# Decoder layer on one core: gather order, expert output buffers and the arithmetic of the last norms

## The chip, the cores and the metric

The kernel runs on one core of a Trainium2 chip. The metric is the time of one execution on the device in microseconds (us); lower is better. A core has five engines that run side by side and wait for each other through semaphores: TensorE (PE in the profile, its weight loads PEld), VectorE (DVE), ScalarE (ACT), GpSimd (POOL) and SyncE (SP), which here only starts transfers. Each engine works through its own queue in order: an instruction that waits holds all that are queued behind it.

## The reference, cut to what matters

One decoder layer on x of 16 x 100 tokens with 512 features: causal self-attention and a layer norm, cross-attention over 16 x 361 context tokens and a layer norm, then a mixture of experts and two norms. The change touches only that last stage:

```python
# x: layer norm of the cross-attention's residual, 1600 tokens x 512
logits = x @ router_w + router_b                  # 8 experts
topk_vals, topk_idx = top_k(logits, 2)
g = softmax(topk_vals)                            # two weights a token
c = sum_j g[j] * silu(x @ expert_w[e_j] + expert_b[e_j])
y = x + c @ proj_w + proj_b
y = norm_w * y / sqrt(mean(y * y) + 1e-6)         # RMS norm
x = x + y
out = (x - mean(x)) / sqrt(var(x) + 1e-5)         # layer norm
```

## The kernel before

Work goes by tiles of 128 tokens (`TT`, 13 tiles, the last of 64). Matrix products are done on pairs: a float32 operand is split into a high part h (a cast on ACT) and a low part l (the difference, on DVE or POOL), and `mm3` issues three matmuls (L145 to L147). `split` is where a pair is made (L137 the cast, L140 the difference).

The experts do not see every token. The gate finds each token's two experts, and each of the 3200 token-expert pairs is given a row in one of 32 slots (`NSL`) of 128 rows, each slot of one expert. The first 11 slots (`EARLY`) are settled before the gate has seen the last tiles; the indices of the others (`idx`, L1247) come later. For slot i:

- `e_gather` (L1261): an indirect DMA, issued by POOL, gathers 128 rows of x (`x2d` in memory) into a buffer of the pool `k_x`.
- `e_turn` (L1270): four PE transposes (tile pte), and the split into the pair xsT (two buffers).
- `e_product` (L1278): 12 matmuls into ph (two PSUM banks), with the expert's weights addressed by a register.
- `e_bias` (L1290): SP loads the expert's bias, broadcast over the partitions (three buffers).
- `e_out` (L1295): DVE adds the bias (L1298), ACT takes Silu (L1299), SP stores the rows to `ysd` in memory (L1300). The result h is written over the gathered rows, so that buffer is free only once the store has landed.

The final stage works on token tile t:

- `f_gather` (L1432): two indirect DMAs fetch the token's two expert rows from `ysd`. They need all slots before `upto(t)` stored: 19 slots for t up to 5, then two more with each tile.
- `f_load` (L1456): z (x plus the projection's bias) and x2.
- `f_sum` (L1475): the weighted sum, on ACT and DVE. `f_turn`, `f_split`: transposes ptc and the pair cp. `f_product`: 12 matmuls into pp.
- `f_square` (L1507): y = pp + z on DVE; ACT squares it and accumulates the sum (L1512); POOL multiplies y by norm_w in place (L1513), which has to come after the square has read y.
- `f_mean` (L1516), and then `f_norm` (L1608): for each step of the list `steps`, one vector of values `V2` goes through a root, `newton` for steps of the first six tiles (`REST`) and `roots` (Sqrt on ACT, a correction on DVE) for later ones. A step holds the RMS value of its own tile and the variance of the tile before. `f_first` adds x2 and takes mean and variance with bn_stats and bn_aggr; `f_second` applies the layer norm and stores.

Before the loop come `e_turn` and `e_product` of slots 0 to 2. The loop over i from 0 to 32 then issues, in program order, `e_gather(i + 4)`, `e_turn(i + 1)`, `e_product(i)`, `e_out(i)`, and what is due: the table `TURN` says in which iteration a final tile's `f_fetch` comes, and `f_prepare`, `f_project` and `f_norm` follow one iteration later each. Tiles from `LATE` on are gathered after the loop, into memory that the experts' weights leave.

The program order isn't the final order. A planner orders each engine's queue by planned times, within the dependencies. `in_turn` adds an order between two instructions of one engine without a semaphore, and `keep_in_program_order` keeps an instruction's place; the gathers have neither. `f_open`, at i = 12, loads and splits proj_w through the three buffers of the pool `stage`, which x2 and other loads use too.

Of the kernel before, what the change touches and what calls it, by code (L numbers as in the profile page):

```python
# [9 lines left out]
FP = mybir.dt.float32  # L10
FR = mybir.dt.float32r
AF = mybir.ActivationFunctionType
# [50 lines left out]
def tile_decoder_layer(  # L63
# [32 lines left out]
    def pool(stack, name, bufs=1, **k):  # L96
        return stack.enter_context(
            tc.tile_pool(name=name, bufs=bufs, reuse_waits="tile", **k)
        )
# [99 lines left out]
    def split_rows(dst, src, name, high=None, low=None):  # L199

        for k in range(KC):
            f = stage.tile([128, D], FP, name=f"f_{name}_{k}", tag="f")
            tc.keep_in_program_order(nc.sync.dma_start(f, src[:, k]))
            split(dst[:, k], f, high, low or nc.gpsimd)
# [7 lines left out]
    def kp(w):  # L212
        return w.rearrange("(k p) n -> p k n", p=128)
# [690 lines left out]
    fin = ExitStack()  # L904
    ctx.enter_context(fin)
    k1 = pool(fin, "k_1", 1, side="right")
    xsp = pool(fin, "k_x", 5, side="right")
    gs = ExitStack()
    gw = pool(gs, "gate", side="right")
    d_l = ExitStack()  # L910
# [347 lines left out]
    ew = Pair(WH, WL).rearrange("p e k n -> p (e k n)")  # L1258
    SLOT, XG, XS, PH = {}, {}, {}, {}

    def e_gather(i):  # L1261
        XG[i] = xsp.tile([128, D], FP, name=f"xs_{i}", tag="xs")
        nc.gpsimd.indirect_dma_start(
            out=XG[i][:],
            out_offset=None,
            in_=x2d[: CUT * 128] if i < EARLY else x2d[:],
            in_offset=bass.IndirectOffsetOnAxis(ap=SLOT[i][0], axis=0),
        )

    def e_turn(i):  # L1270
        xs = XG[i]
        pt = bank("t", [128, KC, 128], f"pte_{i}")
        for k in range(KC):
            nc.tensor.transpose(pt[:, k, :], xs[:, k * 128 : (k + 1) * 128], ident)
        XS[i] = pair(xsp, [128, KC, 128], f"xsT_{i}", tag="xsT", bufs=2)
        split(XS[i], pt)
# [9 lines left out]
        PH[i] = ph  # L1286

    EB = {}

    def e_bias(i):  # L1290
        rv = nc.sync.value_load(SLOT[i][2], min_val=0, max_val=(NE - 1) * D)
# [2 lines left out]

    def e_out(i):  # L1295
        ph = PH.pop(i)
        h = XG.pop(i)
        nc.vector.tensor_tensor(h, ph, EB.pop(i), ALU.add)  # L1298
        nc.scalar.activation(h, h, AF.Silu)  # L1299
        nc.sync.dma_start(ysd[i * 128 : (i + 1) * 128, :], h)  # L1300

    early = [1, 2, 4, 5]
# [107 lines left out]
    def f_open():  # L1410
        gs.close()
        inp["f1"] = pool(f_l, "f_1", 1, side="right")
        inp["f2"] = pool(f_l, "f_2", 3, side="right")
        inp["pw"] = pair(inp["f1"], [128, KC, D], "pw")
        split_rows(inp["pw"], kp(proj_w), "pw")
        inp["nw"] = inp["f1"].tile([128, D], FP, name="nw")
        nc.scalar.dma_start(inp["nw"], norm_w.partition_broadcast(128))

    F, L = {}, {}


    REST, LATE = 6, 8

    TURN = (19, 20, 21, 22, 24, 26, 28, 30)
    BEHIND = 2

    def upto(t):


        return min(NSL, max(EARLY + NE, 2 * (t + 1) + NE - 1))  # L1430

    def f_gather(t):  # L1432
        t0, n = TT[t]
        tail = t >= LATE
        if t == LATE:
            e_l.close()
            w_l.close()
            inp["f3"] = pool(f_l, "f_3", NT - t + 1)
        ys = []
        for j in range(2):  # L1440
            if tail:
                y = inp["f3"].tile([128, D], FP, name=f"y{j}_{t}", tag=f"y{j}")
            else:
                y = inp["f2"].tile([128, D], FP, name=f"y{j}_{t}", tag="y", bufs=6)
            nc.gpsimd.indirect_dma_start(
                out=y[:n],
                out_offset=None,
                in_=ysd[: upto(t) * 128],
                in_offset=bass.IndirectOffsetOnAxis(ap=slot[:n, j, t : t + 1], axis=0),
            )  # L1450
            ys.append(y)
        p = inp["f3" if tail else "f1"]
        cp = pair(p, [128, KC, 128], f"cp_{t}", tag="cp")
        F[t] = ys, cp

    def f_load(t):  # L1456
# [15 lines left out]
    def tiny(n, name, tag, dt=FP):  # L1472
        return inp.get("f3", small).tile([128, n], dt, name=name, tag=tag)

    def f_sum(t):  # L1475
        n = TT[t][1]
        c, y1 = F[t][0]
        tc.keep_in_program_order(
            nc.scalar.activation(c[:n], c[:n], AF.Copy, scale=g1[:n, t : t + 1])
        )  # L1480
        nc.vector.scalar_tensor_tensor(
            c[:n], y1[:n], g2[:n, t : t + 1], c[:n], ALU.mult, ALU.add
        )

    def f_turn(t):
        n = TT[t][1]
        (c, _), cp = F[t]
        pt = bank("s", [128, KC, 128], f"ptc_{t}")
        for k in range(KC):
            nc.tensor.transpose(  # L1490
                pt[:, k, :n], c[:n, k * 128 : (k + 1) * 128], ident[:n, :n]
            )
        F[t] = cp, pt

    def f_split(t):
        n = TT[t][1]
# [9 lines left out]

    def f_square(t):  # L1507
        n = TT[t][1]
        pp, (_, y) = F[t], L[t]
        nc.vector.tensor_tensor(y[:n], pp[:n], y[:n], ALU.add)  # L1510
        ss = tiny(1, f"yss_{t}", "yss")
        nc.scalar.activation(pp[:n], y[:n], AF.Square, accum_out=ss[:n])  # L1512
        nc.gpsimd.tensor_tensor(y[:n], y[:n], inp["nw"][:n], ALU.mult)  # L1513
        F[t] = ss

    def f_mean(t):  # L1516
        n = TT[t][1]
        k = 1.0 if t < REST else 0.25
        nc.vector.tensor_scalar(
            root(0, t)[:n], F[t][:n], k / D, k * EPS_RMS, ALU.mult, ALU.add  # L1520
        )


    steps = [([t], [t - 1] if t else []) for t in range(REST)]
    steps += [
        ([6], [5]),
        ([7, 8], [6]),
        ([9, 10], [7, 8]),
        ([11], [9, 10]),
# [10 lines left out]
    def root(j, t, of=V2):  # L1540

        i, k = where[j, t]
        if i not in V2:
            w = sum(map(len, steps[i]))
            V2[i] = tiny(w, f"sq_{i}", f"sq_{w}")
            if NT - 1 in steps[i][0] + steps[i][1]:
                nc.vector.memset(V2[i], 1.0)
        return of[i][:, k : k + 1]

    def f_first(t):  # L1550

        n = TT[t][1]
        v, r = root(0, t), root(0, t, R2)
        x2, y = L[t]


        if t < REST:
            s = tiny(1, f"s_{t}", "f_s")
            nc.vector.tensor_tensor(s, v, r, ALU.mult)
        else:  # L1560
            s = r
        nc.vector.scalar_tensor_tensor(y[:n], x2[:n], s[:n], y[:n], ALU.mult, ALU.add)  # L1562
        st = tiny(nc.vector.BN_STATS_DIM, f"st3_{t}", "ln_st")
        nc.vector.bn_stats(st[:n], y[:n])  # L1564
        mv = tiny(nc.vector.BN_AGGR_DIM, f"mv3_{t}", "ln_mv")
        nc.vector.bn_aggr(mv[:n], st[:n])
        nc.vector.scalar_tensor_tensor(
            root(1, t)[:n],
            v[:n],
            EPS_LN if t < REST else 4 * EPS_LN,  # L1570
            mv[:n, 1:2],
            ALU.mult,
            ALU.add,
        )
        F[t] = mv

    def f_second(t):
        t0, n = TT[t]
        r = root(1, t, R2)[:n]
        mv, (_, y) = F[t], L[t]  # L1580
        if t == NT - 1:
            nc.vector.tensor_scalar(  # L1582
                y[:n], y[:n], mv[:n, 0:1], r, ALU.subtract, ALU.mult
            )
        else:
            m = tiny(1, f"m3_{t}", "ln_m")
            nc.vector.scalar_tensor_tensor(  # L1587
                m[:n], mv[:n, 0:1], -1.0, r, ALU.mult, ALU.mult
            )
            nc.scalar.activation(y[:n], y[:n], AF.Identity, bias=m[:n], scale=r)  # L1590
        nc.sync.dma_start(out[t0 : t0 + n, :], y[:n])

    def f_fetch(t):
# [13 lines left out]

    def f_norm(i):  # L1608
        v = V2[i]
        if i < REST:  # L1610
            R2[i] = newton(v, f"f_{i}")
        else:
            R2[i] = roots(v, len(steps[i][0]), f"f_{i}")
        for t in steps[i][0]:
            f_first(t)
        for t in steps[i][1]:
            f_second(t)
# [43 lines left out]
    due = {}  # L1661
    for t in range(LATE):
        assert TURN[t] >= upto(t)
        for lag, f in enumerate((f_fetch, f_prepare, f_project, f_norm)):
            if t < REST or lag < 2:
                due.setdefault(min(TURN[t] + lag, NSL), []).append((lag, f, t))
    e_bias(TAIL)
    for i in range(NSL + 1):
        if i + 4 < NSL:
            e_gather(i + 4)  # L1670
        if TAIL < i + 1 < NSL:
            e_turn(i + 1)
            e_bias(i + 1)
        if TAIL <= i < NSL:
            e_product(i)
            e_out(i)
        if i == EARLY + 1:
            f_open()
        for _, f, t in sorted(due.get(i, []), key=lambda d: d[0]):
            f(t)  # L1680
    for t in range(LATE, NT):
        f_gather(t)
    done = REST
    for t in range(REST + 1, LATE):
        f_load(t)
    for k in range(REST, NT + 3):
# [88 lines left out]
```

## Time and profile before

| what | value |
|---|---|
| three runs, median (lowest to highest) | 1432.21 us (1428.25 to 1441.84) |
| the profiled execution, its own time | 1437.28 us |
| its span, first to last instruction | 1435.6 us |
| busy share of the span: PE, PEld | 93%, 77% |
| busy share of the span: DVE, ACT, POOL | 66%, 52%, 51% |
| mean granted TensorE clock | 0.973 |
| the gathers of x (L1263), first to last issue | 1218.8 to 1371.8 us |
| the gathers of expert rows (L1445) | 1322.1 to 1400.1 us |
| last PE matmul starts | 1419.3 us |

Busy shares are averages over all stages. The stages that the change doesn't touch (self-attention, cross-attention, gate) fill the first 1220 us. The change is to be judged in the last 220, stage by stage.

### The profile page before, as it was taken

What the parts mean: (1) busy time and instruction counts of PE and PEld (TensorE: products, weight loads), DVE (VectorE), ACT (ScalarE), POOL (GpSimd) and SP (SyncE); (2) the same over time, 40 slices, a digit from 0 to 9 for tenths busy, and PEclk for the clock granted to TensorE, in tenths of its full rate; (3) what the DMA queues carried; (4) which work ended last, traced back from release to release, by engine and by line L of the source; (5) the groups of instructions that cost most, each with busy time, mean ns of one, the idle gap of its engine ahead of it and who ended that gap; (6) DMA issues with size and microseconds to landing.
All of it is one profiled execution on the core that took longest, in us unless ns stands there. A gap on an engine that the chain in (4) does not pass through costs nothing. (4 is left out here: it accounts for less than half of the span.)

```text
span 1435.6 us, 25188 instructions
## 1 busy us (share of the span) xinstructions
PE 1342.1 (93%) x7952; PEld 1107.7 (77%) x7952; DVE 954.1 (66%) x2978; ACT 746.8 (52%) x1872; POOL 731.1 (51%) x854
## 2 busy tenths in 40 slices
PE   8999989999999999999999999999999897988884
PEld 6888878888778888888888888878887674666663
DVE  5766667775567777777777667767555559653698
ACT  4666643444436666566666566656553232332353
POOL 6877653443335555555555455545444445343542
PEclk9999999999999999999999999999999998899898
DMA  5221254555442232323233222223536554666674
GB/s 157 71 92 53 70 161 111 135 92 110 98 103 62 62 74 51 74 63 75 69 75 70 74 68 69 50 65 76 131 81 200 179 165 129 210 227 214 209 239 139
DMA packets 197873, 159.79 MB, mean 111 GB/s; under 512 B 133322, under 2 KB 152878, under 8 KB 197742
## 3 DMA queue, kind: packets, MB, share of 16 engines
q1 hardware_dynamic: 187904, 137.83, 36.2%
q0 software_dynamic: 4576, 14.95, 3.4%
q10 hardware_dynamic: 5262, 5.41, 1.3%
q8 instruction: 65, 1.06, 0.3%
q14 instruction: 66, 0.54, 0.1%
HBM read 107.16 MB, written 50.99 MB: 110 GB/s over the span
## 5 line engine op out<-in xcount | busy, mean ns | idle before, releaser
L759 POOL TENSOR_SCALAR p<-p,sums 100x361 f32<-100x361 f32 x256 | 146.4, 576 | 100.3 <-DVE sums L758 89.3
L746 DVE CUSTOM_DVE_ANT_0 p<-s,nmask 100x361 f32<-100x361 f32 x256 | 132.9, 527 | 64.7 <-PE s L147 56.2
L757 ACT ACTIVATE p<-p,nm 100x361 f32<-100x361 f32 x256 | 153.2, 602 | 39.8 <-DVE nm L746 36.5
L140 DVE TENSOR_TENSOR pT_l<-ptp,pT_h 128x400 fp32r<-128x400 f32 (+1 forms) x192 | 107.4, 567 | 59.3 <-ACT pT_h L137 58.8
L145 PE MATMUL pq<-WH 128*128 128x512 f32 (+2 forms) x272 | 106.5, 392 | 6.2 <-DVE WH L139 5.8
L767 PE MATMUL ptp<-ident,p 100*128 100x100 f32 (+1 forms) x768 | 107.6, 252 | 0.0
L140 POOL TENSOR_TENSOR cT_l<-cf,cT_h 128x512 fp32r<-128x512 f32 (+1 forms) x48 | 54.4, 1134 | 104.2 <-ACT cT_h L137 102.3
L137 ACT CAST pT_h<-ptp 128x400 fp32r<-128x400 f32 (+1 forms) x192 | 91.3, 487 | 30.2 <-PE ptp L767 29.7
L767 PEld LDWEIGHTS ptp<-ident,p 100*128 100x128 f32 (+1 forms) x768 | 95.6, 152 | 13.5 <-POOL p L759 2.3
L146 PE MATMUL pq<-WL,WH 128*128 128x512 f32 (+2 forms) x272 | 104.1, 383 | 0.0
L147 PE MATMUL pq<-WH,WL 128*128 128x512 f32 (+2 forms) x272 | 103.8, 382 | 0.0
L147 PE MATMUL acc<-WH,ot_l 128*128 128x512 f32 (+1 forms) x208 | 87.3, 421 | 8.7 <-DVE ot_l L140 6.9
L145 PE MATMUL acc<-WH,ot_h 128*128 128x512 f32 (+1 forms) x208 | 87.2, 419 | 5.5 <-ACT ot_h L137 5.5
L145 PE MATMUL s<-kT_h,WH 128*100 128x362 f32 x256 | 88.5, 356 | 2.4 <-ACT kT_h L137 2.4
L145 PE MATMUL av<-pT_h,WH 128*128 128x400 f32 (+1 forms) x192 | 77.1, 401 | 11.6 <-ACT pT_h L137 11.1
L146 PE MATMUL acc<-WL,ot_h 128*128 128x512 f32 (+1 forms) x208 | 85.1, 409 | 0.0
L147 PE MATMUL s<-kT_h,WL 128*100 128x362 f32 x256 | 84.5, 330 | 0.0
L146 PE MATMUL s<-kT_l,WH 128*100 128x362 f32 x256 | 83.9, 328 | 0.0
L614 POOL TENSOR_TENSOR qs<-qs,r_q 128x512 f32<-128x512 f32 (+1 forms) x52 | 54.0, 1068 | 58.0 <-DVE r_q L169 47.5
L140 POOL TENSOR_TENSOR WL<-qf,WH 128x400 fp32r<-128x400 f32 x64 | 67.3, 1051 | 31.0 <-ACT WH L137 27.7
L145 PE MATMUL pv<-WH,cT_h 128*128 128x512 f32 (+1 forms) x192 | 80.0, 417 | 1.3 <-DVE WL L140 1.3
L145 PE MATMUL pk<-WH,cT_h 128*128 128x512 f32 (+1 forms) x192 | 77.7, 405 | 0.2
(330 smaller groups left out, 4030.0 us busy)
## 6 DMA issues: line engine op xcount, KB each, us to landing
qf<-qd SPq DMA_DIRECT2D x64, 200.0 KB
of<-od SPq DMA_DIRECT2D x48, 256.0 KB
cf<-in_ctxT SPq DMA_DIRECT2D x16, 722.0 KB
eb<-in_expert_b SPq DMA_DIRECT2D x32, 256.0 KB
ysd<-xs SPq DMA_DIRECT2D x32, 256.0 KB
f_e<-in_expert_w SPq DMA_DIRECT2D x30, 256.0 KB
f_wq<-in_Wq SPq DMA_DIRECT2D x16, 256.0 KB
f_wo<-in_Wo SPq DMA_DIRECT2D x16, 256.0 KB
```

Source lines behind the costliest of these rows:

```text
L137: ins = nc.scalar.copy(dst.h, src)
L140: low.tensor_tensor(dst.l, src, dst.h.bitcast(FP), ALU.subtract)
L145: nc.tensor.matmul(out, a.h, b.h, start=start, stop=False)
L146: nc.tensor.matmul(out, a.h, b.l, start=False, stop=False)
L147: nc.tensor.matmul(out, a.l, b.h, start=False, stop=stop)
L614: nc.gpsimd.tensor_tensor(qr[:, hs, :], qr[:, hs, :], rs[:n, hs].unsqueeze(2).to_broadcast([n, GR, HD2]), ALU.mult,)
L746: nc.vector.tensor_tensor_reduce(out=p, in0=sc[:, :SE], in1=nmask, scale=1.0, scalar=BIG, op0=ALU.add, op1=ALU.min, accum_out=nm,)
L757: nc.scalar.activation(p, p, AF.Exp, bias=nm, scale=-1.0, accum_out=sh)
L759: nc.gpsimd.tensor_scalar(p, p, sh, 1.0, ALU.mult, ALU.mult)
L767: nc.tensor.transpose(pt[:n, h, :], probs[h][:, c0 : c0 + n], ident[:S, :S])
```

## The change

- Every gather, of x and of expert rows, goes through a new helper `gather`, which keeps all of them on POOL in program order.
- The pool `k_x` has 4 buffers instead of 5. `e_turn` drops its hold on the gathered rows, and `e_out` writes into h, a tile of its own with two buffers.
- The rows of proj_w are loaded one an iteration (i = 13 to 16) by `f_weights`, and each is split an iteration later, its cast ordered behind the last Silu. The low part is now taken by DVE.
- `f_sum`'s ACT instruction is ordered behind the last Silu.
- `LATE` is 9, `TURN` has nine entries: tile 8 is gathered in the loop. The pairs cp of tiles 7 and 8 use the buffers of xsT.
- The first six tiles go through `newton` two at a time, with their variances of the two tiles before: three steps of up to four columns instead of six.
- POOL's product with norm_w is joined with a sum over the row, as one DVE instruction (`tensor_tensor_reduce`). For t from `LATE` on it writes into the tile of the weighted sum. The sum of y gives the mean, x2 having mean zero; bn_stats and bn_aggr go, and the variance is a Square with accumulator on ACT.
- The last tile's final step is on ACT as for the other tiles.

```diff
-    xsp = pool(fin, "k_x", 5, side="right")
+    xsp = pool(fin, "k_x", 4, side="right")
...
+    gathered = [None]
+    def gather(dst, src, idx):
+        ins = nc.gpsimd.indirect_dma_start(
+            out=dst,
+            out_offset=None,
+            in_=src,
+            in_offset=bass.IndirectOffsetOnAxis(ap=idx, axis=0),
+        )
+        gathered[0] = in_turn(ins, gathered[0])
...
     def e_turn(i):
-        xs = XG[i]
+        xs = XG.pop(i)
...
-        h = XG.pop(i)
+        h = ebb.tile([128, D], FP, name=f"h_{i}", tag="h", bufs=2)
         nc.vector.tensor_tensor(h, ph, EB.pop(i), ALU.add)
-        nc.scalar.activation(h, h, AF.Silu)
+        acted[0] = nc.scalar.activation(h, h, AF.Silu)
...
-        split_rows(inp["pw"], kp(proj_w), "pw")
...
+    def f_weights(k):
+        if k < KC:
+            f = stage.tile([128, D], FP, name=f"f_pw_{k}", tag="f")
+            tc.keep_in_program_order(nc.sync.dma_start(f, kp(proj_w)[:, k]))
+            ROW["pw", k] = f
+        if k:
+            f = ROW.pop(("pw", k - 1))
+            in_turn(split(inp["pw"][:, k - 1], f), acted[0])
-    REST, LATE = 6, 8
-    TURN = (19, 20, 21, 22, 24, 26, 28, 30)
+    REST, LATE = 6, 9
+    TURN = (19, 20, 22, 23, 25, 26, 28, 29, 31)
...
+        if REST < t < LATE:
+            cp = pair(xsp, [128, KC, 128], f"cp_{t}", tag="xsT", bufs=2)
...
-        tc.keep_in_program_order(
-            nc.scalar.activation(c[:n], c[:n], AF.Copy, scale=g1[:n, t : t + 1])
-        )
+        ins = nc.scalar.activation(c[:n], c[:n], AF.Copy, scale=g1[:n, t : t + 1])
+        tc.keep_in_program_order(in_turn(ins, acted[0]))
...
-        nc.gpsimd.tensor_tensor(y[:n], y[:n], inp["nw"][:n], ALU.mult)
-        F[t] = ss
+        to = C.pop(t) if t >= LATE else y
+        sn = tiny(1, f"yn_{t}", "yn")
+        nc.vector.tensor_tensor_reduce(
+            out=to[:n], in0=y[:n], in1=inp["nw"][:n], scale=1.0, scalar=0.0,
+            op0=ALU.mult, op1=ALU.add, accum_out=sn[:n],
+        )
...
-    steps = [([t], [t - 1] if t else []) for t in range(REST)]
+    steps = [([t, t + 1], [t - 2, t - 1] if t else []) for t in range(0, REST, 2)]
...
-        nc.vector.bn_stats(st[:n], y[:n])
-        nc.vector.bn_aggr(mv[:n], st[:n])
+        nc.vector.tensor_scalar(nm[:n], F[t][1][:n], -(D**-1.5), None, ALU.mult)
+        nc.scalar.activation(
+            x2[:n], y[:n], AF.Square, bias=nm[:n], scale=D**-0.5, accum_out=var[:n],
+        )
...
-        if t == NT - 1:
-            nc.vector.tensor_scalar(
-                y[:n], y[:n], mv[:n, 0:1], r, ALU.subtract, ALU.mult
-            )
-        else:
-            nc.scalar.activation(y[:n], y[:n], AF.Identity, bias=m[:n], scale=r)
+        nc.vector.scalar_tensor_tensor(m[:n], nm[:n], D**0.5, r, ALU.mult, ALU.mult)
+        nc.scalar.activation(y[:n], y[:n], AF.Identity, bias=m[:n], scale=r)
...
+        if EARLY + 2 <= i < EARLY + 3 + KC:
+            f_weights(i - EARLY - 2)
```

## The prediction

> **What bounds the kernel now.** The change lies in the last 220 us, so after the page's span I read the windows of that part: time, then busy time of PE, PEld, DVE, ACT and POOL with their counts, PE clock, DMA share, GB/s.
>
> ```profile
> span 1435.6 us, 25188 instructions
> ```
> ```profile
> 1250.00:1284.00 34.00, 29.92 (x184) 23.37 (x183) 18.75 (x70) 12.58 (x21) 16.48 (x17) 0.95 0.60 193
> 1284.00:1330.00 46.00, 40.66 (x194) 31.33 (x193) 15.83 (x23) 13.09 (x23) 15.55 (x17) 1.00 0.72 233
> 1330.00:1342.00 12.00, 6.43 (x21) 4.89 (x19) 4.59 (x7) 3.44 (x6) 5.26 (x6) 0.58 0.67 195
> 1342.00:1388.00 46.00, 45.14 (x222) 36.55 (x220) 40.93 (x126) 21.99 (x42) 19.12 (x18) 1.00 0.71 216
> 1388.00:1420.00 32.00, 24.64 (x108) 17.04 (x108) 27.91 (x80) 15.58 (x32) 18.17 (x17) 1.00 0.64 206
> 1420.00:1436.00 16.00, 0.00 (x0) 0.00 (x0) 10.59 (x43) 4.85 (x10) 1.41 (x2) 0.63 0.26 90
> ```
>
> PE is the resource to count, with DVE close behind it from 1342 on. In an undisturbed stretch the timeline starts expert matmuls 0.233 us apart and transposes 0.11 apart, so an expert tile costs PE 12 x 0.233 + 4 x 0.11 = 3.25 us (tiles 16 to 18 begin their transposes at 1301.67, 1304.91, 1308.15), and a final tile (ptc and pp) the same. Counting tiles in the windows gives what PE loses to gaps and to half clock (starts 0.43 apart): 6.5 us of 1250-1284, 6.9 of 1284-1330, 8.3 of 1330-1342, nothing of 1342-1388, 10.1 of 1388-1420. That is 32 us, plus 12.3 us from PE's end (1419.7) to the last DVE instruction (1432.0), and the last store. No gain can exceed about 35 us.
>
> The waits between 1250 and 1390 (total, times, longest) name the causes:
>
> ```profile
> POOL xs L1263 <- DMA ysd<-xs: 26.3, 10, 5.1
> ...
> ACT pw_h L137 <- DMA f_pw<-in_proj_w: 5.6, 1, 5.6
> PE pte L1274 <- DMA xs<-x2d,idx: 4.7, 6, 1.4
> ```
>
> A gather waits until an expert's output has been stored, because output and gathered rows share a buffer; six gathers then reach PE late. The timeline of POOL shows the other trouble (start, duration, idle before and its releaser):
>
> ```profile
> 1320.84 0.94 POOL L1263 DMA_INDIRECT xs<-x2d,idx  x1 [2.12 <-PE pte L1274]
> 1322.09 0.95 POOL L1445 DMA_INDIRECT y<-ysd,slot  x1 [0.30 <-issue]
> ...
> 1328.34 0.95 POOL L1445 DMA_INDIRECT y<-ysd,slot  x1 [0.30 <-issue]
> 1329.59 0.94 POOL L1263 DMA_INDIRECT xs<-x2d,idx  x1 [0.30 <-issue]
> ```
> ```profile
> 1335.97 0.79 PE L145 MATMUL ph<-WH,xsT_h 128*128 x1 [5.57 <-ACT xsT_h L137]
> ```
>
> Six y gathers stand in one run before the xs gather; DVE and ACT then wait for y rows with expert work behind them, and PE has its longest gap of this part. Part of that gap is put down to "remote", and few semaphore records exist there, so its cause is not certain.
>
> **The change, part by part.**
>
> *Own output buffers, four xs buffers.* Gather i+4 now needs the transposes of tile i, not the store of tile i-1. The xs waits on stores go. What is late next at tile 11 is its index: idx is cast at 1271.88, after the gate's chain on DVE, which the change does not touch. A gather takes, by the semaphore updates, 3.3 to 7.2 us from issue to landing, tile 11's own 5.8: rows at 1278.0, then transposes, cast and difference, product 11 at 1279.4, or 1281.4 where product 10 comes after those transposes. It starts at 1284.1 today. The page DMA: Bandwidth & Descriptors of the Trainium skill (Anatomy of one DMA, SWDGE path) fits 2.0 us + bytes / 436e3; for 256 KB that is 2.6 us. By the rule product 11 would start at 1276.2, and today's gathers would hardly be late; the six waits say otherwise, so I take the row. Gain 1250-1284: 2.7 to 4.7, taken **3.5**.
> From 1284 to 1330 the late gathers (1.18 and its echo 1.13, 1.52) and the lesser gaps make 6.9. I take **4** of it as gained.
>
> *The new wait of h.* Two buffers: add i (L1298) waits until store i-2 has landed, and behind it on DVE stand the next xsT_l and, through PSUM's two ph banks, PE. A store's turn is add to store issue (1.4 to 3.4 us) plus landing (2.0 to 6.1, mostly 4): 5.4 typically, against two tiles, 6.5 us. It costs between 0 and 1 us a tile over 8 tiles; I take 0, because the other ph bank covers 2.8 us of such a wait.
>
> *Gathers in program order.* y gathers no longer overtake xs gathers. The first y still waits for the store of tile 18 and lands two gathers later, by my count about 12 us into iteration 19, while the first f_sum stands on ACT behind Silu 20, at about 7.5: ACT is held, xsT_h of tile 22 behind it, and PE waits about 3.7 us plus 1.6 at half clock. 5.3 instead of 8.3: gain 0 to 8, taken **3**.
>
> *The weights of the projection.* The loads go one a turn; casts (4 x 0.61 ACT) stay, the four differences move from POOL (1.29) to DVE (0.69), where 15.8 us of 46 are busy: 2.8 us hidden by PE; without cover, 2.8 lost. ACT's 5.6 us wait goes; it is in the first stage's gain. On SP these loads stand among stores and biases; at one row an iteration they add 0.3 us of queue each.
>
> *norm_w's product on DVE, squares on ACT.* Per tile POOL loses L1513 (1.30). DVE loses bn_stats (0.684) and bn_aggr (0.168), gains the joined product (the two shapes of this operation, 128x128 at 0.29 and 100x361 at 0.527, extrapolate to 0.69 + 0.08 for the accumulator; bounds 0.69 and 0.85) and the nm product (0.15): +0.07, nothing. ACT gains a Square with accumulator, 0.60 + 0.19 as L1512: 10.3 us over 13 tiles, in stages where it is busy 22 of 46 and 16 of 32; where it joins the chain it replaces 0.85 of bn and costs about 0.1 more. The last tile's DVE subtraction (0.54) becomes m (0.15) and an ACT Identity (0.80): +0.45 at the very end.
> What POOL's product costs DVE is visible:
>
> ```profile
> 1401.06 2.53 POOL L1513 TENSOR_TENSOR z<-z,nw 128x512 f32<-128x512 f32 x2
> ...
> 1422.92 1.25 POOL L1513 TENSOR_TENSOR z<-z,nw 64x512 f32<-64x512 f32 x1 [2.76 <-ACT pp L1512]
> ```
> ```profile
> 1401.96 1.65 DVE L1640 TENSOR_TENSOR r_f<-q_f,y_f 128x1 f32<-128x1 f32 x1
> ...
> 1422.95 1.24 DVE L1587 SCALAR_TENSOR_TENSOR m<-mv,r_f 128x1 f32<-128x1 f32 x1
> ```
>
> A one-column instruction of 0.15 us lasts until POOL's product ends. Nine DVE instructions are stretched so, together by 11.0 us over their medians. GPSIMD Engine Reference (Key points) says that POOL shares its SBUF interfaces with DVE and contends with instructions of two SBUF inputs; by it all 13 x 1.30 = 17 us are at risk, by the rows 11.0 are paid. I use the rows: 5.4 of them lie before 1388 under a full PE and bring nothing, 3.5 lie between 1400 and 1411, 2.1 after 1418 on the chain that ends last.
>
> *Roots for two tiles at once.* Three Newton chains fewer, 12 small instructions of about 0.19 us each: 7 us of DVE, all before 1390, where PE is full: no gain, but room for DVE.
>
> *Tile 8 in the loop.* After the last product (1387.8) ten y gathers are issued 1.27 us apart and land 7 to 8 us later; now eight, and tile 8 is ready. With 3.5 us of freed stalls I take half of the 10.1 lost: **5**.
>
> *Tail.* -2.1 (stalls) -0.55 (a DVE with less queued) +0.2 (two Squares for bn) +0.45: **2** gained.
>
> Sum: 3.5 + 4 + 3 + 5 + 2 = 17.5. Profiled, 1437.28 - 17.5 = 1419.8 (span 1435.6 and 1.7 around it). That execution is 5.1 above the median of 1432.21, so for the median I take 1432.2 - 17.5 = **1414.7 us**.
>
> **Rivals.**
> - *More is collected*: the gap at 1330-1342 vanishes wholly (another 5.3), and DVE's room brings 5 more at the end and in the tail: 27.8, 1404. For it: DVE loses 18 us. Against: y 0 still waits for store 18. 0.13.
> - *The first stages give it back*: h's turn comes to 8 us (one store took 6.1 us to land); 4.0 us a tile instead of 3.25 over 8 tiles returns 6, and the gap at 1330 stays, 3: 17.5 - 9 = 8.5, 1424. The same size if the order that the program asks for leaves PE's order as it was. For it: DMA at 0.72. Against: the ph bank's cover. 0.20.
> - *Slower*: in-order f_sum on ACT. Each of the nine tiles in the loop has its y gathers behind an xs gather on one POOL queue (up to 3.75 us) and 5 to 7 us of landing, 9 to 11 us, against two iterations of about 4.8. If y is late by d, ACT holds the next xsT_h, and PE stands d with some 1.3 at half clock. Without harm d is 0 to 1.4, partly covered; from 17.5 / 9 = 1.9 us a tile, d and clock together, the gain is gone; at d = 2.5 it costs 9 x 3.8 = 34: 1449. For it: today's ACT already waits 2.3 for its first y. Against: later y need no fresh store. 0.12.
>
> **How the numbers follow.** The forecast has 0.55. A measurement of this kernel tells about 1%, 14.3 us, from no change: the line is 1417.9. Of the forecast's own spread (1409 to 1421) I put 0.47 under it and 0.08 over; with the first rival 0.60 faster; 0.08 + 0.20 = 0.28 the same; 0.12 slower. The range 1400 to 1434 takes in the two faster rivals and the open gap, and leaves out the slow one and the end of the best.
>
> **Right or wrong in the changed profile.** No xs gather waits on ysd stores; tile 11's product starts at 1279 to 1281; the y gathers lie between xs gathers; no DVE one-column instruction over 1 us after 1340; PE's end about 1404, the tail 10 to 11 us. It is wrong if DVE's L1298 waits for stores, if ACT's f_sum waits at most tiles, or if PE is no longer full between its first and last pp.

## The result and the profile after

The changed kernel takes **1425.13 us** (median of 20 runs, 1419.56 to 1430.0) against 1433.59 for the kernel before, run beside it (20 runs, 1428.25 to 1441.84): ratio 0.9933, 95% interval 0.992 to 0.9946. The medians differ by 8.5 us where 17.5 were forecast. 1425.1 lies inside the range of 1400 to 1434, but the gain is under 1%, where the prediction thought more than 1% likeliest.

The profiled executions differ by 13.5 us of span, but 4.9 of these lie ahead of the first row gather, in stages that the change does not touch (this gather is issued at 1218.8 us before, at 1213.9 after; over the kernels below it moves between 1208 and 1222). From here on stages are counted from that gather. To the end of the span it is 216.8 us before and 208.2 after: 8.6 less, as in the medians.

The windows after, with the borders moved by 4.9 us, and the last three at the same points of the work (time, then busy time of PE, PEld, DVE, ACT and POOL, PE clock, DMA share, GB/s):

```profile
span 1422.1 us, 25158 instructions
```
```profile
1245.10:1279.10 34.00, 30.52 (x191) 24.31 (x190) 18.97 (x71) 11.74 (x19) 13.43 (x15) 0.95 0.67 204
1279.10:1325.10 46.00, 39.92 (x187) 31.80 (x186) 16.91 (x26) 14.94 (x26) 13.23 (x14) 0.95 0.75 237
1325.10:1337.10 12.00, 12.00 (x51) 10.00 (x50) 3.94 (x7) 4.09 (x8) 7.06 (x8) 0.78 0.77 255
1337.10:1375.30 38.20, 38.20 (x192) 31.74 (x191) 31.69 (x92) 22.10 (x46) 12.81 (x14) 1.00 0.78 242
1375.30:1409.60 34.30, 26.62 (x109) 19.06 (x107) 26.32 (x100) 21.95 (x49) 5.59 (x6) 0.90 0.55 182
1409.60:1422.10 12.50, 0.10 (x1) 0.00 (x0) 6.06 (x32) 6.04 (x15) 0.00 (x0) 0.61 0.31 114
```

The hole at 1330-1342 has closed: PE is busy 12.00 us of 12, though at a clock of 0.78; the changed kernel's own gap, 4.0 us, lies just ahead of it, at 1320.6. The last product inside the expert loop ends at 1375.3, 161.4 us after the first gather; before, this point lay at 168.8. That is 7.4 us won. The stretch from there to PE's end, which I call **the late section**, has grown from 32.0 to 34.2 us, with ACT busy 21.95 us of it. Behind PE's end the tail has shrunk from 16.0 to 12.6.

The waits between 1245 and 1390 (total, times, longest), the five that the reading rests on:

```profile
POOL y L1265 <- DMA eb<-in_expert_b: 12.8, 1, 12.8
...
ACT pw_h L137 <- DMA f_pw<-in_proj_w: 7.1, 4, 2.8
ACT pp L1525 <- DMA x<-x2d: 6.3, 1, 6.3
...
PE pte L1281 <- DMA xs<-x2d,idx: 2.1, 2, 1.8
DVE h L1306 <- DMA ysd<-h: 2.1, 1, 2.1
```

No xs gather waits for a store any more, and late rows cost PE 2.1 us, not 4.7. h's new wait shows once. In return ACT stands for the weight rows in four places, 7.1 us (once before, 5.6). The third line's label, a load of x2, is not what ACT waited for: its square at 1384.47 reads a sum of DVE that ended at 1384.38 (more of this under early_loads). The first line is the first y gather; its label names a bias load, but what landed last before it was the store of tile 18, at 1315.3.

### The profile page after: what moved, and what is told of

Read it like the earlier page. It is cut to its first block, busy times and chain, and to the rows that moved or that the text cites. A ratio compares the mean times of both kernels' runs of the same rounds, so it can differ in the third digit from the quotient of the medians.

```text
span 1422.1 us, 25158 instructions
## 1 busy us (share of the span) xinstructions
PE 1338.8 (94%) x7952; PEld 1109.5 (78%) x7952; DVE 939.8 (66%) x2960; ACT 756.9 (53%) x1899; POOL 708.8 (50%) x837
## 3 DMA queue, kind: packets, MB, share of 16 engines
q1 hardware_dynamic: 187904, 137.83, 36.3%
## 4 chain that ended last, share of the span: by engine, by line
PE 69%; DVE 13%; DMA 8%; ACT 4%; issue 3%; POOL 1%; SPq 1%; ACTq 0%; DVEq 0%; POOLq 0%
PE pq L145 4%; PE pq L147 4%; PE pq L146 4%; PE pv L145 4%; PE pv L146 4%; PE pv L147 4%; PE ptp L767 3%; PE pk L145 3%; PE pk L147 3%; PE pk L146 3%; PE s L145 3%; PE s L147 3%; PE s L146 3%; PE av L146 2%; PE av L145 2%
## 5 line engine op out<-in xcount | busy, mean ns | idle before, releaser
L145 PE MATMUL s<-kT_h,WH 128*100 128x362 f32 x256 | 88.2, 355 | 1.7 <-ACT kT_h L137 1.7
```

Source lines behind the costliest of these rows:

```text
L145: nc.tensor.matmul(out, a.h, b.h, start=start, stop=False)
```

## Experiments

Two numbers are read for each kernel: the ratio of its times to those of the kernel before on the same chip, and the stages of one profiled execution from the first gather on. "Against the changed kernel" is the difference of the ratios times 1434 us, with the intervals combined; it takes for granted that a ratio carries from chip to chip. (By it the kernel before stands 9.6 us above the changed one; their medians differ by 8.5.) I call a cause shown only where the timeline shows it and neither number speaks against it.

| kernel | ratio to before (95%) | us against the changed kernel | first gather to span's end | loop ends | late section | tail |
|---|---|---|---|---|---|---|
| before | 1 | +9.6 | 216.8 | 168.8 | 32.0 | 16.0 |
| changed | 0.9933 (0.992-0.9946) | 0 | 208.2 | 161.4 | 34.2 | 12.6 |
| own_only | 0.9961 (0.9947-0.9974) | +4.0 ± 2.7 | 211.8 | 156.6 | 38.3 | 16.9 |
| pool_product | 0.9996 (0.9978-1.0014) | +9.0 ± 3.2 | 213.7 | 160.8 | 36.8 | 16.1 |
| bn_on_dve | 0.9934 (0.9909-0.996) | +0.1 ± 4.1 | 206.7 | 159.6 | 35.2 | 11.9 |
| late8 | 0.998 (0.9961-0.9998) | +6.7 ± 3.2 | 207.6 | 157.1 | 35.9 | 14.6 |
| no_chain | 0.9919 (0.9896-0.9942) | -2.0 ± 3.8 | 210.7 | 161.4 | 35.6 | 13.7 |
| y0_later | 0.9925 (0.9899-0.9951) | -1.1 ± 4.2 | 210.2 | 160.3 | 36.3 | 13.6 |
| warm11 | 0.9933 (0.9909-0.9957) | 0 ± 3.9 | 207.8 | 159.7 | 34.3 | 13.8 |
| early_loads | 0.9912 (0.9887-0.9936) | -3.0 ± 4.0 | 201.9 | 158.8 | 30.5 | 12.6 |
| pw_lag2 | 0.991 (0.9889-0.9931) | -3.3 ± 3.5 | 205.2 | 155.7 | 35.9 | 13.6 |
| combo1 | 0.9883 (0.9854-0.9912) | -7.2 ± 4.6 | 196.2 | 152.9 | 27.6 | 15.7 |
| combo2 | 0.9897 (0.9868-0.9925) | -5.2 ± 4.5 | 197.8 | 151.8 | 29.7 | 16.3 |
| combo_cold | 0.9882 (0.9849-0.9916) | -7.3 ± 5.1 | 207.7 | 159.9 | 36.2 | 11.6 |

The stage columns need care, because the traces are of two kinds. In seven of them, which I call **clean** (pool_product, bn_on_dve, late8, early_loads, pw_lag2, combo1, combo2), PE's signal that a product or some transposes are done is recorded within 0.02 us of their end. In the other seven (before, changed, own_only, no_chain, y0_later, warm11, combo_cold) there are stretches of several us with next to no signals on record, and in them an engine goes on only up to 8.4 us after PE's work that it waits for has ended. These are real waits of that execution. Whether the chip or the taking of the profile makes them is not known; the kind goes with the chip of the run (14 and 5 clean, 2 and 3 not). Stages of a clean and of another trace can differ by this alone: up to the end of product 23 early_loads does the same as the changed kernel, and its trace is 2.6 us ahead there.

### One part alone: own output buffers (own_only)

```
 before:  xsp = pool(fin, "k_x", 5 -> 4, side="right")
          xs = XG[i]  ->  xs = XG.pop(i)                                   (e_turn)
          h = XG.pop(i)  ->  h = ebb.tile([128, D], FP, name=f"h_{i}", tag="h", bufs=2)
```


> The kernel before with one part of the change alone: expert outputs in two buffers of their own, xs buffers four. Gathers in the old order, norm on GpSimd, tile 8 after the loop, weights cast in one block. The prediction gave this part 3.5 us up to tile 11 and 4 us up to 1330: 7.5 us less than before (216.8 us from the first row gather's issue to the span's end would become 209). Theory 'idle turns to half clock': PE waits for gather 11, which hangs on its index, runs the next tile at half clock, and only 2 to 4 us are kept. A further rival: what is gained is lost again to the y gathers' wait for the store of tile 18: 0 to 1 us.

Measured: 5.6 us less than before by the times (0.9961), 5.0 by the profile. The windows from the first gather to the loop's last product, the late section, and the tail:

```profile
1221.30:1377.90 156.60, 147.27 (x734) 116.51 (x732) 94.74 (x289) 60.70 (x111) 70.23 (x69) 0.93 0.74 232
1377.90:1416.20 38.30, 28.93 (x109) 19.62 (x108) 27.84 (x82) 16.78 (x35) 17.36 (x16) 0.87 0.53 171
1416.20:1433.10 16.90, 0.12 (x1) 0.00 (x0) 11.41 (x43) 4.85 (x10) 2.25 (x2) 0.61 0.25 85
```

The loop ends 12.2 us sooner than before (168.8 to 156.6), and also sooner than in the changed kernel as a whole (161.4). Up to the start of product 22 it is 7.4 us ahead (107.1 to 99.7), which is the 7.5 that the prediction gave this part; the rest comes at the hole of before. But the late section grows by 6.3 us (32.0 to 38.3), with the same 109 matmuls in it. It is not a block of fixed length that moves up with the loop.

### The norm's edit undone (pool_product, bn_on_dve)

```
 after:  tensor_tensor_reduce(z * nw, sum)              ->  gpsimd.tensor_tensor(z, z, nw, mult)
         tensor_scalar(nm), activation(Square -> var)   ->  bn_stats, bn_aggr     (bn_on_dve: only this line)
```


> The changed kernel with the whole of the norm's edit undone: product with norm_w on GpSimd, bn_stats and bn_aggr on DVE, no added Square; roots in pairs, gathers, own buffers and tile 8 in the loop stay. The prediction's terms: 3.5 us of stretched DVE instructions in the late section and 2.1 in the tail come back, 1430 to 1431. Rival: the stretched instructions were covered, and what the edit gives is lost on ACT again: 1424 to 1426.

> The changed kernel with the variance of the last norm taken by bn_stats and bn_aggr on DVE again, as before the change; the product with norm_w stays joined to a DVE sum (the sum itself is not used). ACT loses 13 Squares of 0.71 + 0.19 us, DVE gains 13 x (0.85 - 0.15) = 9 us. Theory 'ACT queue': ACT is what is late after 1389 (casts and sums behind Squares), so 2 to 3 us are gained: 1422 to 1423. Theory 'late loads': the first wait of the late section stays, DVE, busy 26 of 34 us there, gets 4 more: 1425 to 1428.

pool_product gives back 9.0 ± 3.2 us by the times and 5.5 by the profile (forecast 5.6). Its timeline of DVE, and that of POOL, at the same moment (start, duration):

```profile
1388.16 0.74 DVE L1576 SCALAR_TENSOR_TENSOR z<-x,s,z 128x512 f32<-128x512 f32 x1
1388.82 3.25 DVE L1494 SCALAR_TENSOR_TENSOR y<-y,g,y 128x512 f32<-128x512 f32 x1
1391.99 0.68 DVE L1523 TENSOR_TENSOR z<-pp,z 128x512 f32<-128x512 f32 x1
```
```profile
1388.96 2.54 POOL L1526 TENSOR_TENSOR z<-z,nw 128x512 f32<-128x512 f32 x2
```

A DVE sum of 0.75 us lasts 3.25 while two products run on POOL. Seven DVE instructions after 1335 are stretched so, by 7.0 us together; in the changed kernel and in bn_on_dve there is none. bn_on_dve says which half of the edit mattered: with the variance on DVE again, nothing is lost (0.1 ± 4.1 us). These two runs, both with clean traces, differ by 8.9 us in the times and by 7.0 in the profile. So the gain is the product's leaving POOL; moving the squares to ACT is not seen in the time, and the theory that ACT's added Squares set the late section is not borne out.

### Tile 8 (late8)

```
 after:  REST, LATE = 6, 9 -> 6, 8        TURN = (19, ..., 28, 29, 31) -> (19, ..., 28, 29)
```


> The changed kernel with final tile 8 after the loop again, as before the change; all else stays. The prediction counted on tile 8 in the loop, with the stalls, for 5 us between the last expert product and PE's end: by it the section grows from 34.2 to 36 to 38 us and the kernel by 1.5 to 4 us. Theory 'late loads': what holds this section is the loads of z and x2, issued after the last product for tile 8 in either place; the gathers are not what is late, so PE's end moves by less than 1.5 us either way.

The numbers disagree. By the times tile 8 in the loop is worth 6.7 ± 3.2 us; in the profile the sum is the same (207.6 and 208.2): the loop ends 4.3 us sooner without it, and the late section and the tail are 1.7 and 2.0 longer. The two traces are of different kinds. The profiled execution took 1428.8 us, where the median of its 14 runs is 1432.2. That it gains is likely; how much of it lies in the late section stays open.

### Order of the gathers, and the first y (no_chain, y0_later)

```
 no_chain:  gathered[0] = in_turn(ins, gathered[0])  ->  gathered[0] = ins
 y0_later:  for t == 0, f_prepare and f_project one expert tile later
```


> The changed kernel without the order asked of the gathers: the planner puts the row gathers of tiles 24 and 25 in front of the first y gathers again. Prediction: the order is worth 3 us, so 3 us longer than the changed kernel (208.2 from the first row gather to the span's end becomes 211). Theory 'one queue, one wait': in the changed kernel the first y gather stands 12.8 us on GpSimd until the store of tile 18 has landed, and row gathers 24 and 25 behind it; with these two ahead the order is worth nothing or costs: 0 to 2 us shorter.

> The changed kernel with the sum, transposes and product of final tile 0 one expert tile later; its gathers stay. Theory 'fresh store': ACT stands 6.2 us for the first y rows with the cast of tile 23 behind it, PE loses 4.2 us and runs 6.8 us at half clock; one tile (3.25 us) later ACT waits some 3 us less and PE's gap falls to 1 to 2: 3 to 5 us shorter than the changed kernel (208.2 becomes 203 to 205). Rival: row gathers 24 and 25 stand behind the y gathers on GpSimd and become the next wait, at once: 0 to 1.5 us shorter.

The order alone cannot be told from nothing: -2.0 ± 3.8 by the times, +2.5 by the profile. In the changed kernel the first y gather holds POOL's queue, and f_sum holds ACT. The timelines of POOL and of ACT:

```profile
1302.63 0.94 POOL L1265 DMA_INDIRECT xs<-x2d,idx  x1 [2.26 <-PE pte L1281]
1316.36 0.94 POOL L1265 DMA_INDIRECT y<-ysd,slot  x1 [12.78 <-DMA eb<-in_expert_b]
1317.61 0.95 POOL L1265 DMA_INDIRECT y<-ysd,slot  x1 [0.30 <-issue]
1318.86 0.95 POOL L1265 DMA_INDIRECT xs<-x2d,idx  x1 [0.30 <-issue]
```
```profile
1323.10 0.72 ACT L1492 ACTIVATE y<-y,g 128x512 f32<-128x512 f32 x1 [6.24 <-issue]
1323.72 0.56 ACT L137 CAST xsT_h<-pte 128x512 fp32r<-128x512 f32 x1
```

The cast of tile 23 stands right behind the late y sum. y0_later takes this wait from ACT, and PE waits all the same, now for row gather 24, which stands behind the y gathers on POOL (issued at 1321.04; PE's wait for it ended at 1327.63). Its timeline of PE:

```profile
1322.27 0.39 PE L147 MATMUL ph<-WH,xsT_l 128*128 x1
1327.73 1.09 PE L1281 MATMUL pte<-ident,xs 128*128 128x128 f32 x4 [5.08 <-issue]
```

The rival of that run holds: one wait was put in another's place, and there is no gain (-1.1 ± 4.2).

### Half clock at tile 11 (warm11)

```
 after, in e_turn:  for _ in range({11: 18, 12: 5}.get(i, 0)): transpose(pt[:, 0, :], ident, ident)
```


> The changed kernel with PE kept busy while it waits for row gathers 11 and 12: 18 and 5 transposes of the identity ahead of these tiles' own (0.11 us each, 2.5 us in all), into PSUM that the own transposes then overwrite. Theory 'idle turns to half clock': PE's product 11 took 5.7 us instead of 2.9 because PE had stood 3.6 us before it; with PE busy it runs at full clock, product 12 starts 2 to 3 us sooner and the kernel is 2 to 3 us shorter. Rival 1: the clock falls all the same; 0, or 0.5 us longer. Rival 2: the clock holds, but the casts of the weight rows and the first y gather take it back: product 12 sooner, the end within 1 us.

In the changed kernel PE waits for gather 11, and product 11 starts at 1276.38; by the clock of before that is 1281.3, just past the forecast's 1279 to 1281. But it runs at half speed (matmuls 0.43 us apart) and takes 5.9 us up to the next transposes, not 2.9. Four windows of the changed kernel, 3.4 us each:

```profile
1269.00:1272.40 3.40, 2.98 (x14) 2.13 (x12) 0.69 (x1) 0.63 (x1) 2.35 (x3) 1.00 0.83 246
1272.40:1275.80 3.40, 1.26 (x8) 0.84 (x8) 1.38 (x2) 1.40 (x3) 0.94 (x1) 1.00 0.99 326
1275.80:1279.20 3.40, 2.48 (x5) 1.61 (x6) 0.69 (x1) 0.20 (x1) 0.95 (x1) 0.50 0.78 202
1279.20:1282.60 3.40, 3.40 (x10) 2.52 (x10) 0.03 (x1) 0.00 (x0) 0.00 (x0) 0.50 0.33 129
```

A stretch with PE busy 1.26 us of 3.4 is followed by two at 0.50. The transposes of the identity push product 10 into the gap; PE keeps clock 1.00 there, and product 12 starts 66.0 us after the first gather, not 68.9: 2.9 us, as the theory said. At tile 18 they are gone (88.3 and 88.2), and the time is unchanged. So the half clock is shown as what tile 12 loses, and in the profile it does not set the end; the times (0 ± 3.9 us) could hide 2.9. Rival 2 fits.

### The casts of the weight rows (pw_lag2)

```
 after, f_weights:  if k: cast row k - 1  ->  if k > 1: cast row k - 2
```


> The changed kernel with the rows of the projection's weights cast two expert tiles after their load is asked for, not one. Theory 'rows late': a row takes 5.2 to 6.2 us from issue to landing against 3.25 for a tile, ACT stands at three casts (7.1 us in all) and PE loses 1.90 and 0.49 us at 1307 and 1311: gain 2 to 2.5, 1422.5 to 1423. Rival: what comes after (the first y gather waits for the store of tile 18, and that store moves with the tiles) gives it back, or the casts only move in front of another tile's: 1424.5 to 1425.5.

What takes the 2.9 us: rows of proj_w land 4.5 to 6.2 us after their issue and are cast in the next turn, 3.25 us later. ACT of the changed kernel, then PE:

```profile
1305.21 0.62 ACT L137 CAST pw_h<-f_pw 128x512 fp32r<-128x512 f32 x1 [2.84 <-DMA f_pw<-in_proj_w]
1305.74 0.58 ACT L137 CAST xsT_h<-pte 128x512 fp32r<-128x512 f32 x1
```
```profile
1307.30 0.47 PE L145 MATMUL ph<-WH,xsT_h 128*128 x1 [1.74 <-DVE h L1306]
```

Cast a turn later, the rows are there. ACT of pw_lag2, at the corresponding casts:

```profile
1305.99 0.60 ACT L137 CAST pw_h<-f_pw 128x512 fp32r<-128x512 f32 x1
1307.49 0.59 ACT L137 CAST xsT_h<-pte 128x512 fp32r<-128x512 f32 x1 [0.89 <-PE pte L1281]
```

Product 23 then ends 5.1 us sooner (112.0 for 117.1), the loop 5.7 sooner; the late section gives back 1.7, the tail 1.0. Against early_loads, a clean trace like this one, product 23 ends 2.5 us sooner and the loop 3.1. By the times the gain is 3.3 ± 3.5, in line with the 3.0 of the profile, but not apart from nothing.

### The loads of z and x2 (early_loads)

```
 after, f_load:  if REST < t < LATE: z, x2 = two xsp tiles, tag "xs"; the loads go on SP
                 in the loop, at i = NSL - 2, in place of ACT's queue after the loop
```


> The changed kernel with one thing moved: the loads of z and x2 for tiles 7 and 8 go on SP before the last two expert tiles, into xs buffers that the gathers no longer need, instead of on ACT's queue after the last product (issued from 1377.6, landed at 1381.6 to 1385.0). Theory 'late loads': these loads are what holds DVE's add (4.1 us) and through it ACT (6.3 us), PSUM and PE (2.9 us and the half clock behind it) between 1375 and 1389; with them gone the section from the last expert product to PE's end falls from 34.2 to 30 to 31.5 us and the kernel to 1421 to 1422.5. Rival 'ACT queue': the section is held by ACT's added Squares and Identities in front of casts and sums; the next wait comes at once, PE's end moves by less than 1 us, 1424 to 1425.

ACT of the changed kernel at the start of the late section, then DVE, then PE:

```profile
1377.58 0.34 ACTq L1484 DMA_DIRECT2D z<-xbd  x1
...
1378.93 0.44 ACTq L1484 DMA_DIRECT2D x<-x2d  x1
1384.47 0.60 ACT L1525 ACTIVATE pp<-z 128x512 f32<-128x512 f32 x1 [6.31 <-DMA x<-x2d]
```
```profile
1383.69 0.69 DVE L1523 TENSOR_TENSOR z<-pp,z 128x512 f32<-128x512 f32 x1 [4.09 <-PE pp L147]
```
```profile
1379.43 0.39 PE L147 MATMUL pp<-pw_h,cp_l 128*128 128x512 f32 x1
1382.15 0.39 PE L147 MATMUL pp<-pw_h,cp_l 128*128 128x512 f32 x1
1385.25 0.79 PE L145 MATMUL pp<-pw_h,cp_h 128*128 128x512 f32 x1 [2.71 <-ACT pp L1525]
1385.84 0.63 PE L146 MATMUL pp<-pw_l,cp_h 128*128 128x512 f32 x1
```

Tiles 7 and 8 find their gathered rows ready, but z and x2 are asked for only at 1377.58, when the last product has freed the memory for them. When I set the run up I took ACT's label at its word and held these loads for the cause. The rows do not bear that out. DVE's add at 1383.69 is the seventh of thirteen, that of tile 6, and tile 6's z was loaded in the loop (issued at 1370.11, landed at 1373.8). Its product ended at 1379.82 (the first PE line), and DVE still waited for PE's signal, recorded at 1383.66: the delay described under the table. ACT's square waits for this add, PE for the PSUM bank, and the next matmuls are 0.42 us apart. DVE's check for tile 7's z came at 1386.11 and held nothing up.

In early_loads the signal comes at once, and the late section is 30.5 us, as forecast (30 to 31.5):

```profile
1372.40:1402.90 30.50, 24.90 (x109) 18.09 (x107) 26.34 (x101) 21.95 (x49) 5.89 (x6) 0.94 0.52 175
```

But so it does in bn_on_dve, whose loads are as late as the changed kernel's. The adds of tiles 6 and 7 there:

```profile
1386.63 0.69 DVE L1523 TENSOR_TENSOR z<-pp,z 128x512 f32<-128x512 f32 x1 [0.25 <-PE pp L147]
1389.72 0.69 DVE L1523 TENSOR_TENSOR z<-pp,z 128x512 f32<-128x512 f32 x1
```

From the loop's end to the end of tile 10's product bn_on_dve takes 19.3 us, early_loads 19.2 and the changed kernel 22.9. So the 3.7 us that the late section lost are not shown to be the loads' doing: the forecast number came, but by luck. Of the 6.3 in all, 2.6 were there before the edit does anything. The times (-3.0 ± 4.0) are not apart from nothing, and the profiled execution was the fastest of its six.

The loads do hold a kernel whose loop ends sooner. In pw_lag2, a clean trace, tile 7's z landed at 1383.02, 4.9 us after that tile's product had ended, and PE then waits 3.0 us and runs 6.8 us at half clock:

```profile
1383.11 0.69 DVE L1523 TENSOR_TENSOR z<-pp,z 128x512 f32<-128x512 f32 x1 [2.74 <-DMA z<-xbd]
```

The rival, ACT's queue, is not supported either: ACT and DVE have the same work in early_loads as in the changed kernel (21.95 and 26.34 us).

### Together (combo1, combo2, combo_cold)

combo1 joins early_loads, pw_lag2 and warm11. combo2 adds f_sum one tile sooner after the loop (k + 3 for k + 2). combo_cold is combo1 without warm11's transposes.

> The changed kernel with the three edits tried one by one put together: z and x2 of tiles 7 and 8 loaded early, weight rows cast two tiles after their load, PE kept busy ahead of tiles 11 and 12. From the first row gather to the span's end the changed kernel takes 208.2 us; early loads alone took 6.3 off (3.7 of them in the last section), late casts 3.0, busy PE 0.4. Theory 'next wait': each was taken back because another wait came next, so together they give at least their sum and the 2.9 us that the full clock freed: 196 to 199. Rival: DVE and ACT, each with some 25 us of work in the last 34, end the section at the same moment however soon it begins: 201 to 204.

> The same with the sums of final tiles 9 to 12 asked for one tile sooner. In the changed kernel PE stands 3.2 us before the transposes of tile 11 for its sum on DVE, which stands behind a Square and two Identities on ACT; the rows had landed 10 us before. With the sums sooner this wait goes and PE's end comes 2 to 3 us sooner than with the three edits. Rival: the sums take DVE's and ACT's time from the casts of tiles 8 to 10, and the gap moves there: within 1 us.

> The three edits together without the transposes that keep PE busy: early loads and late casts only. Alone, busy PE freed 2.9 us at tile 12 and had lost them by tile 18, where PE waits for ACT with the casts. Theory: with the casts out of the way these 2.9 us reach the end, so without them 196.2 becomes 198 to 200. Rival: tile 18 comes at the same moment all the same, since another wait (the store of tile 18, then row gather 24 behind the first y gathers) takes them: 196 to 197.

combo1, in windows that end with the loop, PE and the span:

```profile
1329.10:1372.80 43.70, 43.70 (x217) 36.30 (x216) 32.85 (x95) 24.08 (x50) 16.51 (x17) 1.00 0.89 294
1372.80:1400.40 27.60, 25.44 (x113) 18.72 (x111) 24.55 (x92) 19.94 (x44) 8.24 (x8) 0.94 0.59 191
1400.40:1416.10 15.70, 0.14 (x1) 0.00 (x0) 8.25 (x40) 8.47 (x19) 0.00 (x0) 0.61 0.25 92
```

It takes 1417.9 us beside 1435.5 for the kernel before, and its interval (0.9854 to 0.9912) lies wholly under that of the changed kernel: this version beats both. In the profile the loop ends at 152.9 and PE at 180.5 us after the first gather, 15.1 sooner than in the changed kernel; 3.1 of it are lost in the tail. That is 12.0 us, more than the 9.7 of the three edits one by one, and inside the 196 to 199 of "next wait". But the changed kernel's trace and warm11's are not clean, and by the times it is 7.2 ± 4.6 against a sum of 6.3, so that the whole is more than its parts is not shown. Against pw_lag2, also clean, the late section falls from 35.9 to 27.6 us and the times by 3.9 ± 5.1.

combo2 gains nothing on it (0.9897 against 0.9883): PE's wait ahead of tile 11 goes, and waits for casts of tiles 8 and 9 come, as its rival said. combo_cold has the time of combo1 (0.9882), so the busy PE is not shown to be worth anything there either, and the early loads and late casts together are: -7.3 ± 5.1. Its profiled execution is much longer (207.7; 1417.8 in all, where the median of its runs is 1413.3). The trace is not clean: an ACT cast starts at 1319.77, 7.4 us after the transposes that it reads, with 10.2 us of half clock from 1319 on, and although its loads are early the late section is 36.2. It cannot be set beside combo1's, and the question of that run stays open in the profile.

## Why the prediction was half right

By its own steps:

- **1250 to 1284, 3.5 us.** Right as a mechanism: no gather waits for a store, and tile 11 hangs on its index (gather issued at 1267.2, landed at 1273.6). Tile 9 starts 5.0 us sooner and tile 11 2.8. The sum left out what the wait for the gather does to the clock: tile 12 starts 0.3 us later than before.
- **1284 to 1330, 4 us.** The term for the buffers was right: alone they bring the start of product 22 7.4 us nearer (3.5 + 4 forecast). What failed is the step beside it, "the weights of the projection", costed as hidden, with 0.3 us of queue. A row lands 4.5 to 6.2 us after its issue and is used 3.25 after it; ACT stands 7.1 us for the four, and in pw_lag2 product 23 ends 5.1 us sooner (2.5 against a clean trace). My line on ACT's 5.6 us wait of the kernel before ("goes") was wrong: it became four waits of 7.1 us, one stage later. Gain up to the start of product 18: 4.4, against 7.5; of product 22: 3.4.
- **h's new wait, 0.** Right: one wait of 2.1 us on DVE, none of PE's charged to it. In pw_lag2 it shows seven times, 8.0 us in all, and the loop is faster all the same. Three buffers were not tried, since they leave no room for f_2.
- **y gathers, 3 us.** The picture of the changed kernel was nearly right: ACT held 6.2 us, PE 4.0; but 6.8 us at half clock cost about 3.4 us, not 1.6 (half of them, an estimate). The hole of the kernel before, with which it was compared, was misread. In the trace of before the first y rows held DVE to 1328.94 only; then DVE's add of expert tile 21 stood for a product that had ended at 1326.05, and ACT's cast of tile 23 for transposes that had ended at 1326.95:

```profile
1326.35 0.60 PE L1274 MATMUL pte<-ident,xs 128*128 128x128 f32 x4
```
```profile
1333.08 0.69 DVE L1298 TENSOR_TENSOR xs<-ph,eb 128x512 f32<-128x512 f32 x1 [3.39 <-remote]
```
```profile
1335.33 0.58 ACT L137 CAST xsT_h<-pte 128x512 fp32r<-128x512 f32 x1 [7.87 <-remote]
```

  This is PE's late signal again, and most of the 8.3 us hang on it, not on the order of the gathers, which no_chain shows to be worth nothing measurable. From product 22's start to the end of product 23 the lead grows from 3.4 to 5.4 us. y0_later shows that the sum on ACT is only the first of two waits in that place.
- **norm_w on DVE, 5.6 us of freed DVE.** Right: 5.5 in the profile, 9.0 ± 3.2 in the times. In the profile 2.6 of it lie in the late section (3.5 in the prediction) and 3.5 in the tail (2.1), less 0.6 ahead of them; between the two clean traces, with and without the product on POOL, it is 7.0. The joined product takes 0.68 + 0.08 us (estimate 0.69 + 0.08); the Square 0.71 + 0.19 (0.60 + 0.19).
- **Late section, 5 us.** **This step failed.** It took half of the 10.1 us lost there as gained, from two gathers fewer and freed stalls. Both happened, and the section became 2.2 us longer. What PE stands for instead differs from trace to trace. In the changed kernel it is PE's late signal at tile 6 (2.7 us and 3.4 at half clock), then tile 11's sum, which waits on DVE (the first line below). In bn_on_dve, as fast by the times and clean, the first of these is missing and the section is still 35.2 us: the wait ahead of tile 11 is longer (the second line), with 10.2 us of half clock. In pw_lag2 it is the load of z.

```profile
1401.28 1.10 PE L1503 MATMUL ptc<-ident,y 128*128 128x128 f32 x8 [3.05 <-DVE nm L1592]
```
```profile
1406.99 1.71 PE L1503 MATMUL ptc<-ident,y 128*128 128x128 f32 x8 [5.72 <-DVE y L1494]
```

  The error was to add a shorter section to an earlier start. I had read the ten gathers as that section's wait and had not looked at what else is waited for there. How much of the 5 us a trace free of late signals would show stays open, since neither before nor the changed kernel has one.
- **Tail, 2 us.** 3.4: the stall at the end went; what the last tile's ACT step costs is not seen apart.

Of the rivals, the second named 8.5 us and came out at that number by luck, not by its mechanism: h's store turn was harmless. Of its other half, the gap at the first y, 4.0 us are still there. "More is collected" came true only with the loads and the casts moved, in combo1. "Slower" is out: f_sum waits at the first tile only. Of the prediction's own signs, PE's end came at 1409.5 (1414.4 by the clock of before, for about 1404) and the tail at 12.6 (for 10 to 11); and one sign of being wrong came true: PE is busy 26.6 us of the 34.3 of the late section, so it is not full up to its last final product.

## What to carry to other kernels

A gain in a stage reaches the end only as far as what the next stage waits for came sooner too; before gains are added, ask of each later stage which load, buffer or index it would then be waiting for, and measure a part alone at the point where its stage ends as well as at the kernel's end. A transfer issued one turn ahead needs a turn longer than its landing; if it is shorter, the engine that consumes it in order hands the wait to everything behind it. A wait's label names the signal that came last on record: compare the end of the work waited for with the start of the one who waits, and compare a stage only between traces that agree there. Buffers that fall idle ahead of a stage (here the gather's) are a place for that stage's first loads, once the loop ends soon enough to wait for them, as in pw_lag2 and combo1.

## What the runs showed of the hardware

PE's clock fell after a wait that had no long gap in it: the single gaps before 1276.4 were 1.75, 0.38 and 1.00 us with transposes between them. The page TensorE: Matmul & The Clock Gate of the Trainium skill (Why this matters for your kernels) asks for no idle gap over some 3 us; here 1.26 us of work in a stretch of 3.4 was too little, and with 2.5 us of transposes of a constant ahead of it the clock stayed at 1.00. The times of half clock in the last 200 us of these traces, up to PE's last matmul, are 3.4, 6.8 or 10.2 us long, so a short wait can cost a whole tile its speed. And POOL's two-input product held one DVE sum for 3.25 us, longer than any seen before the change (2.20), with two products in a row on POOL. In seven of fourteen traces engines went on up to 8.4 us after the PE work that they waited for had ended, in the other seven PE's signal was never more than 0.02 us late; the cause is open.
